# A three-group sigmoid recurrence with ten warm-up steps instead of twelve, the first of them without a product

## The chip, the cores and the metric

The kernel runs on one core of one Trainium2 chip. The metric is the device time of one execution, in microseconds; the median of three runs of the kernel before is 1776.05 (1774.83 to 1778.08).

## The reference, cut to what matters

`x` is 8 images of 128 channels and 48 x 48 = 2304 tokens, all fp32. Layer 0 is group norm, a causal attention over the tokens and a residual; layer 1 normalises the tokens, runs a full attention and adds it. Both attentions are left as they are by the change. What follows them is the feed-forward part, a recurrence over the tokens:

```python
def _L1_ffn_ref(x, W, V, gamma, beta):
    B, T, H = (x.shape[0], x.shape[1], W.shape[0])        # 8, 2304, 128
    Wx = jnp.einsum('bti,hi->bth', x, W)
    flat = Wx.reshape(B * T, H)
    mean = jnp.mean(flat, axis=0); var = jnp.var(flat, axis=0)
    Wx = ((flat - mean) * jax.lax.rsqrt(var + BN_EPS) * gamma + beta).reshape(B, T, H)
    Vt = V.T
    def step(yt, wx_t):
        yt = jax.nn.sigmoid(wx_t + yt @ Vt)
        return (yt, yt)
    y0 = jnp.zeros((B, H), dtype=Wx.dtype)
    _, ys = jax.lax.scan(step, y0, jnp.swapaxes(Wx, 0, 1))
    return jnp.swapaxes(ys, 0, 1)
...
t = t + _L1_ffn_ref(_ln_t(t), L1_ffn_W, L1_ffn_V, L1_ffn_gamma, L1_ffn_beta)
```

`V` is orthogonal, and a sigmoid's slope is at most a quarter, so the state forgets where it began in a few steps.

## The kernel before, in words

There are two parts, one after the other, in the function `fast_path`.

The first part, nearly all of the time, is the two attentions of eight images. TensorE's work is a list, `stream`, written out by hand: for each item a product of scores (L1013 causal, L1214 full), and three items later the product with the values (L1024, L1228, L1224). Between them a small planner, `Stream`, places chains of short steps (projections, norms, transposes, residuals) by stated costs and due times. The schedule is manual: each engine executes its instructions in the order in which they are recorded. The constants of the recurrence come in early. `ffn_weights` (L743 to L751) is one such step, put in with a due time of 30 us: DVE takes the row means off the weights `w1` (L746 to L748), TensorE transposes it into one PSUM bank `tp_ffn` (L750), and DVE copies it out as `w1T` (L751). `vT_f`, the transposed `V`, is loaded from memory (L740).

The second part is the recurrence (L1443 on). The 2304 tokens of each image are cut into 96 segments of LS = 24 tokens, so that all segments of all images go through the 24 steps at once. The 96 segments form G = 3 groups of 32, and a step of one group is a 128 x 256 tile (8 images x 32 segments). A segment doesn't know the state that the one before it ends with, so each starts WARM = 12 tokens earlier, in the tail of the segment before, from a state of 0.5 (`y0`, L1506 and L1507). The step is: DVE writes the scaled inputs of two steps into a PSUM bank (`inputs`, L1488 to L1502: one instruction for groups 1 and 2, and in the warm-up two for group 0, whose first segment has no segment before it); TensorE adds `V y` into the bank (L1547, an fp32 product, so two matmul records); ACT takes the sigmoid out of PSUM (L1549). The three groups take turns on each engine. Group 0's first segment begins at the first token, so its warm-up is discarded: its state is set to 0 (L1552). At the end `seams` (L1515) compares the state at which each segment ends with the warmed-up state at which the next began; if any differs by over 1e-5, a flag sends the program into `general_path`, which computes everything again.

Around the loop: TensorE clears six banks with products of zeros (L1475) and fills a wait with products that nobody reads (`idle`, L1477 and L1395), and makes a small product for the flag (L1533) ahead of the first step. The queue of SP loads the residuals (L1462 and L1464) and later stores the results (L1530). GpSimd adds the residuals (L1529) from step 1 on, and issues adding stores for group 0 (L1562). The last four steps' residuals are added by DVE.

Of the kernel before, what the change touches and what calls it, by code (L numbers as in the profile page):

```python
# [14 lines left out]
F32 = mybir.dt.float32  # L15
AF = mybir.ActivationFunctionType
ALU = mybir.AluOpType
# [8 lines left out]
SEGS = 96  # L26
# [578 lines left out]
def fast_path(ctx: ExitStack, tc: tile.TileContext, x, pe, w_ffn, out, x_tok, w_qkv, w_pos, v_t, gamma_beta, flag):  # L605
    nc = tc.nc
    B, C, H, W = x.shape
    N = H * W
    P = 128
# [15 lines left out]
    LS = N // SEGS  # L625
# [27 lines left out]
    w1T = cpool.tile([P, P], F32, tag="w1T", name="w1T")  # L653
    vT_f = cpool.tile([P, P], F32, tag="vT_f", name="vT_f")
    gb = cpool.tile([P, 2], F32, tag="gb", name="gb")

    def rsqrt(pool, out_ap, var_ap, eps, tag):

# [5 lines left out]
    with ExitStack() as actx:  # L664
# [78 lines left out]
        def ffn_weights():  # L743

            s = small.tile([P, 1], F32, tag="gn_d", name="w_sum")
            nc.vector.tensor_reduce(s, w1, AX.X, ALU.add)  # L746
            nc.vector.tensor_scalar_mul(s, s, 1.0 / P)
            nc.vector.tensor_scalar(w1, w1, s, None, ALU.subtract)  # L748
            tp = psum_t("tp_ffn")
            nc.tensor.transpose(tp[:, 0:P], w1, ident)  # L750
            nc.vector.tensor_copy(w1T, tp[:, 0:P])  # L751


        same = apool.tile([P, R, SQ], F32, tag="same", name="same")
# [685 lines left out]
        order.close()  # L1440


    WARM = 12  # L1443
    G = SEG_GROUPS
    TZ = 2
    TO = [4] + [2] * (G - 1)
    assert LS * SEGS == N and WARM % TZ == 0 and LS % TO[0] == 0 and SG * B * TZ == CH
    with ExitStack() as rctx:
        rc = rctx.enter_context(tc.tile_pool(name="rconst", bufs=1))
        rst = [rctx.enter_context(tc.tile_pool(name=f"rst{g}", bufs=4 if g == 0 else 6)) for g in range(G)]  # L1450
        rres = rctx.enter_context(tc.tile_pool(name="rres", bufs=6))
        rlast = rctx.enter_context(tc.tile_pool(name="rlast", bufs=4))
        ps_z = [rctx.enter_context(tc.tile_pool(name=f"ps_z{g}", bufs=2, space=PSUM)) for g in range(G)]
        ps_w = rctx.enter_context(tc.tile_pool(name="ps_w", bufs=1, space=PSUM))

        rctx.enter_context(tc.manual_schedule())


        t2s = [None] + [rc.tile([P, B, LS, SG], F32, tag=f"t2s_{g}", name=f"t2s_{g}") for g in range(1, G)]
        for g in range(1, G):  # L1460
            for b in range(0, B, 4):
                nc.sync.dma_start(t2s[g][:, b : b + 4], t2s_d[:, g - 1, b : b + 4])  # L1462
        t2l = rc.tile([P, LS - LM, B, SG], F32, tag="t2l", name="t2l")
        nc.sync.dma_start(t2l, t2l_d)  # L1464

        zero = rc.tile([P, CH], mybir.dt.bfloat16, tag="zero", name="zero")
        nc.gpsimd.memset(zero, 0.0)
        pw = ps_w.tile([P, CH], F32, tag="w", name="pw")

        zs = [deque() for _ in range(G)]  # L1470
        banks = [deque() for _ in range(G)]
        for t in range(-WARM, -WARM + 2 * TZ, TZ):
            for g in range(G):
                z = ps_z[g].tile([P, TZ, B, SG], F32, tag="z", name=f"z_{g}_{t}")
                nc.tensor.matmul(z.rearrange("p t b s -> p (t b s)"), zero[:, :P], zero, start=True, stop=True)  # L1475
                banks[g].append(z)
        idle(pw[:, 2 * P :], 8)  # L1477

        mv = rc.tile([P, 2], F32, tag="bn_mv", name="bn_mv")
        nc.vector.bn_aggr(mv, stats)  # L1480
        a = rc.tile([P, 1], F32, tag="bn_a", name="bn_a")
        rsqrt(rc, a, mv[:, 1:2], 1e-5, "bn")
        nc.vector.tensor_mul(a, a, gb[:, 0:1])
        c = rc.tile([P, 1], F32, tag="bn_c", name="bn_c")
        nc.vector.tensor_mul(c, mv[:, 0:1], a)
        nc.vector.tensor_sub(c, gb[:, 1:2], c)

        def inputs(g, t):  # L1488


            z = banks[g].popleft() if banks[g] else ps_z[g].tile([P, TZ, B, SG], F32, tag="z", name=f"z_{g}_{t}")
            s0 = g * SG
            if t >= 0:
                nc.vector.tensor_scalar(z, wx[:, t : t + TZ, :, s0 : s0 + SG], a, c, ALU.mult, ALU.add)
            else:
                before = wx[:, LS + t : LS + t + TZ]
                if g:
                    nc.vector.tensor_scalar(z, before[:, :, :, s0 - 1 : s0 + SG - 1], a, c, ALU.mult, ALU.add)
                else:
                    nc.vector.tensor_scalar(z[:, :, :, 1:], before[:, :, :, : SG - 1], a, c, ALU.mult, ALU.add)  # L1500
                    nc.vector.tensor_scalar(z[:, :, :, 0:1], before[:, :, :, 0:1], a, c, ALU.mult, ALU.add)
            return z  # L1502

        prev, warm, y = [], [], [None] * G
        for g in range(G):
            y0 = rc.tile([P, B, SG], F32, tag=f"y0_{g}", name=f"y0_{g}")  # L1506
            nc.gpsimd.memset(y0, 0.5)  # L1507
            prev.append(y0)
            warm.append(rc.tile([P, B, SG], F32, tag=f"warm_{g}", name=f"warm_{g}"))
            zs[g].append(inputs(g, -WARM))  # L1510

        d = rc.tile([P, G, B, SG], F32, tag="d", name="d")
        dm = rc.tile([P, G], F32, tag="dm", name="dm")

        def seams(g):  # L1515

            n = SG if g < G - 1 else SG - 1
            nc.vector.tensor_sub(d[:, g, :, : SG - 1], prev[g][:, :, : SG - 1], warm[g][:, :, 1:])
            if n == SG:
                nc.vector.tensor_sub(d[:, g, :, SG - 1 :], prev[g][:, :, SG - 1 :], warm[g + 1][:, :, 0:1])  # L1520
            nc.vector.tensor_reduce(dm[:, g : g + 1], d[:, g, :, :n], AX.XY, ALU.max, apply_absolute_value=True)

        ys = {}

        def add_residual(g, l0, yt):
            engine, pool = (nc.gpsimd, rres) if l0 < LM - TZ else (nc.vector, rlast)
            r = pool.tile([P, TZ, B, SG], F32, tag="r", name=f"r_{g}_{l0}")
            t2 = t2s[g].rearrange("p b l s -> p l b s")[:, l0 : l0 + TZ] if g else t2l[:, l0 - LM : l0 - LM + TZ]
            engine.tensor_add(r, yt, t2)  # L1529
            nc.sync.dma_start(out[g, :, l0 : l0 + TZ], r)  # L1530


        nc.tensor.matmul(pw[0:1, :B], ones[:, 0:1], bound, start=True, stop=True)  # L1533
        fl = rc.tile([1, 4], F32, tag="fl", name="fl")
        nc.vector.reduce_max(fl[:, 0:1], pw[0:1, :B], AX.X)
        nc.vector.tensor_scalar(fl[:, 1:2], fl[:, 0:1], LOGIT_BOUND / SCALE, None, ALU.is_gt)

        for t in range(-WARM, LS):
            s = t % TZ
            for g in range(G):  # L1540
                if s == 0 and t + TZ < LS:
                    zs[g].append(inputs(g, t + TZ))
                so = t % TO[g]
                if so == 0:
                    y[g] = rst[g].tile([P, TO[g], B, SG], F32, tag="y", name=f"y_{g}_{t}")
                z = zs[g][0]
                nc.tensor.matmul(z[:, s], vT_f, prev[g], start=False, stop=True, skip_group_check=True)  # L1547
                to = warm[g] if t == -1 else y[g][:, so]
                nc.scalar.activation(to, z[:, s], AF.Sigmoid)  # L1549
                prev[g] = to  # L1550
                if t == -1 and g == 0:
                    nc.vector.memset(warm[0][:, :, 0:1], 0.0)  # L1552
                if s == TZ - 1:
                    zs[g].popleft()

                    l0 = t + 1 - TZ
                    ys[g, l0] = y[g][:, so + 1 - TZ : so + 1]
                    if 0 <= l0 and (g or l0 >= LM):
                        if l0 < LM - TZ:
                            add_residual(g, l0, ys[g, l0])  # L1560
                    elif l0 >= 0 and so == TO[0] - 1:
                        nc.gpsimd.dma_start(out[0, :, t + 1 - TO[0] : t + 1], y[0], accum_op=ALU.add)  # L1562
                if t == LS - 1:
                    seams(g)
                elif t == LM + 1 and g:
                    add_residual(g, LM - TZ, ys[g, LM - TZ])

        off = rc.tile([P, 1], F32, tag="off", name="off")
        nc.vector.tensor_reduce(off, dm, AX.X, ALU.max)
        nc.vector.tensor_scalar(off, off, STATE_TOL, None, ALU.is_gt)  # L1570
        for k, (l0, g) in enumerate((l, g) for l in range(LM, LS, TZ) for g in range(G)):
            add_residual(g, l0, ys[g, l0])
            if k:
                continue
            nc.tensor.matmul(pw[0:1, P : P + 1], off, ones[:, 0:1], start=True, stop=True)
            nc.vector.tensor_scalar(flag, pw[0:1, P : P + 1], fl[:, 1:2], 0.5, ALU.add, ALU.is_gt)
# [56 lines left out]
```

## Time and profile before

| | |
|---|---|
| median of three runs | 1776.05 us (1774.83, 1776.05, 1778.08) |
| profiled execution, first to last instruction | 1772.5 us |
| what lies around it, against that median | 3.58 us |
| TensorE granted clock, mean | 0.993 |
| recurrence, from its first product to the last sigmoid | 1710.25 to 1757.2 us |
| stores and flag after that, to the end | 15.3 us |
| TensorE products L1547 in the warm-up | 12 steps x 3 groups |

Times inside the profile are from the span's start. Each row of the timeline is the start, how long it took, the engine, the line, the operation, the tile written and the tiles read, the number of instructions merged, and in brackets how long the engine had been idle and what released it. PE stands for TensorE, PEld for its weight loads, DVE for VectorE, ACT for ScalarE, POOL for GpSimd, SP for SyncE. The runs' times are of other executions than the profiled one; no time of its own is recorded for that beside its span.

### The profile page before, as it was taken

Reading aid. Unit: us, or ns where it says so; the run is one execution under the profiler, and the core shown is the slowest. Engines: PE = TensorE matmul, PEld = TensorE weight load, DVE = VectorE, ACT = ScalarE, POOL = GpSimd, SP = SyncE. Lnnn points to the kernel's source line nnn. Section 1 sums busy time; section 2 is a strip of 40 time slices with the busy share of each in tenths; the row PEclk is TensorE's granted clock in tenths of the full one; section 3 lists DMA queues with packets and bytes.
Section 4 is the critical chain, followed back from the end, with each engine's and each line's share of the span. In section 5 each row is a group of like instructions: output and inputs, shape, how many; then the busy total and the mean of one; then the engine's idle time right before and its main releaser. Section 6 shows DMA issues by size and latency. Waiting matters only on the chain.

```text
span 1772.5 us, 22223 instructions
## 1 busy us (share of the span) xinstructions
PE 1742.7 (98%) x6231; PEld 1093.2 (62%) x6231; DVE 1302.8 (74%) x3363; ACT 764.8 (43%) x1842; POOL 195.2 (11%) x303
## 2 busy tenths in 40 slices
PE   8999999999999999999999999999999999999996
PEld 5666566665666566665666656665666656665565
DVE  4868668876887668786687767876687866877467
ACT  2344434443345434444344433454344543444455
POOL 1110011100110001100111001100011001110006
PEclk8999999999999999999999999999999999999998
DMA  4405672257533584156732575335941468116768
GB/s 140 138 23 187 182 204 94 87 184 188 145 103 128 159 226 141 34 176 182 200 99 80 188 192 152 106 111 161 237 129 50 160 183 214 45 65 198 194 211 216
DMA packets 206056, 262.00 MB, mean 148 GB/s; under 512 B 90113, under 2 KB 175010, under 8 KB 205412
## 3 DMA queue, kind: packets, MB, share of 16 engines
q1 hardware_dynamic: 204972, 257.47, 49.4%
q0 software_dynamic: 720, 2.62, 1.0%
q8 instruction: 52, 0.85, 0.2%
q14 instruction: 80, 0.66, 0.1%
q10 hardware_dynamic: 232, 0.40, 0.1%
HBM read 150.24 MB, written 110.17 MB: 147 GB/s over the span
## 4 chain that ended last, share of the span: by engine, by line
PE 96%; DMA 1%; DVE 1%; ACT 0%; issue 0%; SPq 0%; POOL 0%; ACTq 0%; POOLq 0%; DVEq 0%
PE o L1228 18%; PE s L1214 18%; PE s L1013 17%; PE o L1024 17%; PE o L1224 13%; PE pj L874 4%; PE pj L877 2%; PE z L1547 2%; PE wx L1320 2%; PE of_t L934 1%; PE tb L934 1%; PE pb L832 0%; DMA x<-in_x_dram 0%; PE dn L1072 0%; PE ts L1259 0%
## 5 line engine op out<-in xcount | busy, mean ns | idle before, releaser
L1216 ACT ACTIVATE p<-s,shift 128x384 f32<-128x384 f32 x504 | 292.4, 580 | 479.7 <-PE s L1214 464.2
L1015 ACT ACTIVATE p<-s 128x384 f32<-128x384 f32 (+2 forms) x504 | 231.8, 460 | 424.8 <-PE s L1013 377.5
L1214 PE MATMUL s<-xh 128*128 128x384 f32 x1008 | 410.4, 489 | 0.0
L1228 PE MATMUL o<-p,xhT 128*128 128x384 f32 x1008 | 404.1, 488 | 5.9 <-ACT p L1216 5.9
L1013 PE MATMUL s<-q,k 128*128 128x384 f32 (+2 forms) x1008 | 381.5, 460 | 0.2 <-DVE k L884 0.2
L1024 PE MATMUL o<-p,vT 128*128 128x384 f32 (+2 forms) x1008 | 377.4, 456 | 0.0
L1224 PE MATMUL o<-g,xhT 128*128 128x384 f32 x720 | 281.3, 488 | 1.1 <-DMA g<-e 1.1
L1228 PEld LDWEIGHTS o<-p,xhT 128*128 128x128 f32 x1008 | 188.9, 190 | 133.8 <-ACT p L1216 10.5
L1024 PEld LDWEIGHTS o<-p,vT 128*128 128x128 f32 x1008 | 188.8, 190 | 114.7 <-issue 0.6
L1214 PEld LDWEIGHTS s<-xh 128*128 128x128 f32 x1008 | 186.2, 190 | 115.3
L1013 PEld LDWEIGHTS s<-q,k 128*128 128x128 f32 x1008 | 182.6, 191 | 97.3 <-issue 1.0
L1039 DVE TENSOR_TENSOR acc<-acc,p 128x384 f32<-128x384 f32 (+2 forms) x408 | 208.8, 512 | 33.4 <-POOL p L1018 8.7
L1177 DVE STREAM_TRANSPOSE t<-p 128x384 f32<-128x384 f32 x360 | 187.3, 550 | 37.6 <-ACT p L1216 32.8
L1224 PEld LDWEIGHTS o<-g,xhT 128*128 128x128 f32 x720 | 133.2, 190 | 83.7 <-DMA g<-e 1.3
L1185 DVE TENSOR_REDUCE tsum<-t 128x12 f32<-128x1152 f32 x120 | 162.3, 1353 | 4.2
L879 DVE TENSOR_TENSOR z<-pj,pb 128x384 f32<-128x384 f32 x144 | 78.8, 547 | 108.8 <-PE pj L874 92.4
L1018 POOL TENSOR_TENSOR p<-p,triu 128x128 f32<-128x128 f32 x144 | 72.5, 505 | 606.2 <-ACT p L1015 475.2
L1294 POOL TENSOR_TENSOR roots<-ve_f,mhalf 128x3 f32<-128x3 f32 x48 | 40.7, 849 | 521.8 <-DVE ve_f L918 521.8
L1216 ACT ACTIVATION_READ_ACCUMULATOR p<-s,shift 128x1 f32 x504 | 97.2, 193 | 0.0
L874 PE MATMUL pj<-xn,wT 128*128 128x384 f32 x192 | 79.7, 500 | 1.4 <-DVE xn L867 1.4
L924 POOL TENSOR_TENSOR rs_c<-ve_c,mhalf 128x3 f32<-128x3 f32 x48 | 45.1, 939 | 216.2 <-DVE ve_c L918 213.6
L1321 DVE TENSOR_TENSOR scale<-wx,scale 128x384 f32<-128x384 f32 x46 | 25.4, 551 | 56.1 <-PE wx L1320 50.3
(264 smaller groups left out, 1485.6 us busy)
## 6 DMA issues: line engine op xcount, KB each, us to landing
e<-t SPq DMA_DIRECT2D x120, 576.0 KB
g<-e SPq DMA_DIRECT2D x480, 144.0 KB
pb<-posb_d SPq DMA_DIRECT2D x46, 576.0 KB
t1t<-in_x_tok_dram SPq DMA_DIRECT2D x48, 192.0 KB
t_d<-tt SPq DMA_DIRECT2D x184, 48.0 KB
t2x<-t_d SPq DMA_DIRECT2D x46, 192.0 KB
scale<-rs SPq DMA_DIRECT2D x46, 192.0 KB
x<-in_x_dram SPq DMA_DIRECT2D x14, 576.0 KB
```

What stands on the lines that cost most here:

```text
L874: nc.tensor.matmul(ps[:, :QC], wT[:, j, :], xn, start=True, stop=True)
L879: nc.vector.tensor_add(z, ps[:, :QC], c["pb"][:, j, :])
L1013: nc.tensor.matmul(s[:, off:QC], keys[b][:, ts(m, P)], queries[b, j][:, off:], start=True, stop=True)
L1015: nc.scalar.activation(p[:, off:], s[:, off:QC], AF.Exp, scale=SCALE)
L1024: nc.tensor.matmul(o[:, off:QC], vals[b][:, ts(m, P)], p[:, off:], start=first, stop=last)
L1039: nc.vector.tensor_add(a[:, off:], a[:, off:], p[:, off:])
L1177: nc.vector.transpose(t[:, :, :, g, :].rearrange("p b j r -> p j b r"), p.rearrange("p (j b r) -> p j b r", j=QB, b=R))
L1185: nc.vector.tensor_reduce(self.tsum[j][:, n - j - 1, :], t.rearrange("p b j m r -> p (b j) (m r)"), AX.X, ALU.add)
L1214: nc.tensor.matmul(s[:, :QC], xh[:, ts(m, P)], xh[:, ts(j, QC)], start=True, stop=True)
L1216: nc.scalar.activation(p, s[:, :QC], AF.Exp, bias=shift, accum_out=self.rows[:, m, j : j + 1])
L1224: nc.tensor.matmul(out_ap, xhT[:, QB * i + g, :], p, start=first, stop=last)
L1228: nc.tensor.matmul(o[:, :QC], xhT[:, what[1], :], p, start=first, stop=last)
```

## The change

The warm-up is ten steps. In its first step, the state before it is a constant, 0.5 in every element, so `V y` is the same column for every token: half the row sums of `V`. That column, `v_half`, is computed once (a product of `vT_f` with a column of 0.5, in the bank `tp_ffn` that the transposed weights also use), copied to SBUF, and given to the first sigmoid as its bias. So the first step has no product, and the three tiles `y0` with their fills are gone. Group 0's warm-up inputs become one instruction: the tile is read one element earlier, so the first segment of each image reads some other element, and what comes of it is discarded as before.

```diff
+    half = cpool.tile([P, 1], F32, tag="half", name="half")
+    nc.gpsimd.memset(half, 0.5)
+    v_half = cpool.tile([P, 1], F32, tag="v_half", name="v_half")
...
             nc.tensor.transpose(tp[:, 0:P], w1, ident)
             nc.vector.tensor_copy(w1T, tp[:, 0:P])
+            nc.tensor.matmul(tp[:, P : P + 1], vT_f, half, start=True, stop=True)
+            nc.vector.tensor_copy(v_half, tp[:, P : P + 1])
...
-    WARM = 12
+    WARM = 10
...
-                before = wx[:, LS + t : LS + t + TZ]
-                if g:
-                    nc.vector.tensor_scalar(z, before[:, :, :, s0 - 1 : s0 + SG - 1], a, c, ALU.mult, ALU.add)
-                else:
-                    nc.vector.tensor_scalar(z[:, :, :, 1:], before[:, :, :, : SG - 1], a, c, ALU.mult, ALU.add)
-                    nc.vector.tensor_scalar(z[:, :, :, 0:1], before[:, :, :, 0:1], a, c, ALU.mult, ALU.add)
+                at = (LS + t) * B * SEGS - 1
+                before = wx.rearrange("p l b s -> p (l b s)")[:, at : at + TZ * B * SEGS]
+                before = before.rearrange("p (l b s) -> p l b s", l=TZ, b=B)[:, :, :, s0 : s0 + SG]
+                nc.vector.tensor_scalar(z, before, a, c, ALU.mult, ALU.add)
...
-            y0 = rc.tile([P, B, SG], F32, tag=f"y0_{g}", name=f"y0_{g}")
-            nc.gpsimd.memset(y0, 0.5)
-            prev.append(y0)
+            prev.append(None)
...
-                if so == 0:
+                if so == 0 or t == -WARM:
                     y[g] = rst[g].tile([P, TO[g], B, SG], F32, tag="y", name=f"y_{g}_{t}")
                 z = zs[g][0]
-                nc.tensor.matmul(z[:, s], vT_f, prev[g], start=False, stop=True, skip_group_check=True)
                 to = warm[g] if t == -1 else y[g][:, so]
-                nc.scalar.activation(to, z[:, s], AF.Sigmoid)
+                if t > -WARM:
+                    nc.tensor.matmul(z[:, s], vT_f, prev[g], start=False, stop=True, skip_group_check=True)
+                    nc.scalar.activation(to, z[:, s], AF.Sigmoid)
+                else:
+                    nc.scalar.activation(to, z[:, s], AF.Sigmoid, bias=v_half)
```

## The prediction

> **What bounds the kernel now.** I read four views: the page's part 4 first (what the end depends on), then the chain of waits over the recurrence, the timeline of the two places that the diff touches, and the busy times by stretch.
>
> The chain that ended last lies on TensorE nearly everywhere, so a TensorE microsecond saved or added anywhere should reach the end, unless a wait takes it up:
>
> ```profile
> PE 96%; DMA 1%; DVE 1%; ACT 0%; issue 0%; SPq 0%; POOL 0%; ACTq 0%; POOLq 0%; DVEq 0%
> ```
>
> The chain at the start of the recurrence (start, length, what):
>
> ```profile
> 1710.19 0.12 PE pw L1533 x2
> 1710.32 0.63 PE z_-12_14294 L1547 x2
> 1710.95 0.44 PE z_-12_14296 L1547 x2
> 1711.44 0.67 PE z_-12_14298 L1547 x2
> 1712.11 0.43 PE z_-12_14294 L1547 x2
> ...
> 1718.69 0.43 PE z_-6_14383 L1547 x2
> 1719.13 0.43 PE z_-6_14389 L1547 x2
> ```
>
> From 1712.11 on, a group's step takes 0.43 us of TensorE, a step of three groups 3 x 0.432 = 1.296 us. TensorE is the limit, not the loop through ACT, which would give 0.59 + 0.38 us. Only the first round is slower (1710.32 to 1712.11, 1.79 us): it waits for DVE's first inputs, as the timeline shows.
>
> ```profile
> 1708.72 0.80 DVE L1500 TENSOR_SCALAR z_-12_14294<-wx,bn_a,bn_c 128x496 f32<-128x496 f32 x1
> 1709.55 0.31 DVE L1501 TENSOR_SCALAR z_-12_14294<-wx,bn_a,bn_c 128x16 f32<-128x16 f32 x1
> 1709.77 0.81 DVE L1498 TENSOR_SCALAR z_-12_14296<-wx,bn_a,bn_c 128x512 f32<-128x512 f32 x1
> 1710.48 0.81 DVE L1498 TENSOR_SCALAR z_-12_14298<-wx,bn_a,bn_c 128x512 f32<-128x512 f32 x1
> ```
>
> DVE's instructions of 0.81 us start 0.71 us apart; group 0's two cost 0.83 + 0.22 us.
>
> The other place is at 30 us, where `v_half` is put. TensorE stands still there already, waiting for DVE's weight means, and its clock then falls:
>
> ```profile
> 28.11 0.49 PE L1013 MATMUL s<-q,k 128*128 128x128 f32 x2
> ...
> 30.09 0.43 PE L750 MATMUL tp_ffn<-ident,w 128*128 128x128 f32 x1 [1.50 <-DVE w L748]
> ...
> 30.56 0.29 DVE L751 COPY w1T<-tp_ffn 128x128 f32<-128x128 f32 x1 [0.52 <-PE tp_ffn L750]
> ```
>
> Busy times by stretch (length; PE, PEld, DVE, ACT, POOL; granted clock, DMA share, GB/s):
>
> ```profile
> 29.00:30.00 1.00, 0.00 (x0) 0.00 (x0) 0.93 (x4) 0.00 (x0) 0.65 (x1) 1.00 1.00 410
> 31.00:32.00 1.00, 1.00 (x3) 0.64 (x2) 0.00 (x0) 0.00 (x0) 0.00 (x0) 0.50 0.36 143
> 1725.00:1730.00 5.00, 5.00 (x24) 4.26 (x23) 4.53 (x8) 4.36 (x12) 0.80 (x1) 1.00 0.00 0
> 1735.00:1740.00 5.00, 5.00 (x25) 4.39 (x24) 4.30 (x7) 4.42 (x13) 5.00 (x6) 1.00 1.14 294
> ```
>
> **What the Trainium skill says.** "TensorE: Matmul & The Clock Gate", Part 1: the clock is halved after an idle window of about 3.4 us and restored after a busy one, and the windows run freely, so their place differs between executions. The trace agrees on the length: the clock is 0.50 from 30.3 to 33.7 us. It is stricter on the cause: 1.5 us without a product was enough here. "ScalarE: Activation LUTs", What ACT_TABLE_LOAD costs: a bias given as a 128 x 1 operand adds about 93 ns to an ACTIVATE. The trace agrees: the exponential with a bias takes 580 ns (L1216, 128x384), the one without 490 ns (L1015's 128x384 form).
>
> **The change part by part.**
>
> 1. *Three rounds of products leave TensorE*: 12 rounds become 9, at 1.296 us: -3.89 us if the new start is as good as steady state.
>
> 2. *The new start.* DVE's chain up to 1708.70 is untouched. Group 0's first input is now one instruction, ready at 1709.53; groups 1 and 2 follow at 1710.24 and 1710.95. ACT can take the first sigmoids straight after these (0.04 us to notice, 0.38 + 0.09 us long): 1710.04, 1710.75, 1711.46. TensorE is not free before 1710.32, since the fillers and L1533 stand ahead of the first product in its queue, so the first product of step -9 starts at 1710.32, just where step -12 started before; group 2's ends at about 1712.2. The next inputs follow on DVE after L1535 and L1536 (two times 0.18 us): from 1711.11 on, ready at 1711.92, 1712.63 and 1713.34. TensorE's second round therefore waits for groups 1 and 2 (1712.75 and 1713.46, a product after a wait lasting 0.67 us, as at 1711.44) and ends at 1714.13. Two rounds on, step -6 begins at 1714.13 + 1.296 = 1715.42. Before, it began at 1718.69. Gain: 3.27 us. So 0.62 of the 3.89 us is given back to DVE's start, and the bias's 3 x 0.09 us lies behind DVE's waits.
>
> 3. *One instruction less per pair of steps on DVE* (1.05 to 0.71 us, 0.34): DVE needs 2.14 us per 2.59 us of TensorE instead of 2.48, so nothing comes of it past the start. If the shifted read were slower than the 0.81 us of groups 1 and 2, which it equals in form, there are 0.45 us of room.
>
> 4. *After the warm-up* all work follows the steps. GpSimd's first addition comes at 1729.20, released by a sigmoid, and is idle before; DMA moves nothing from 1725 to 1730 and the residual loads are in by about 1724, before the first addition's new time of 1725.9. The stores, which then fill the DMA engines, start that much earlier: I pass on all 3.27 us. The three fills of `y0` (0.31 us each on GpSimd) and the fill of `half` lie where GpSimd waits: nothing. No DMA is added or moved, and no queue of SP changes its order.
>
> 5. *`v_half` at 30 us.* In the changed program the new product waits for the copy L751, which reads the same bank, and stands ahead of L874 in TensorE's queue; behind it wait all later products. So: L750 ends at 30.52; 0.04 us to DVE, 0.29 us copy, 0.04 us back: 30.89. The product's two passes with a 128 x 128 weight and one column: the nearest row is the group norm's (L799), 0.56 us on the chain at 10.72, also at half clock. L874 begins at 31.44 instead of 30.52: +0.92 us. Does this pass on? The chain runs from here over TensorE to 43.43, over DVE to 48.04 and over TensorE again; DVE's idle time before 43.45 is a wait for that same L874 of TensorE, so I take all of it. Bounds: 0.21 us (the like product L1072 amid full-clock work: 0.12 us, and 0.09 us more for its successor), if the wait were covered; 0.67 us with the clock full; and above, a second window at half clock, which takes half of 3.41 us, 1.71 us, more. The copy to `v_half` (0.15 us, as L801) lies in DVE's wait for `pb` that ends at 35.98: nothing.
>
> Sum: -3.27 + 0.92 = -2.35 us. The profiled execution goes from 1772.5 to 1770.1 us; with 3.58 us around it, which is how the median stands to it, 1776.05 becomes **1773.7 us**, 0.13% less. The measurement can tell about 0.2% (3.6 us) from no change.
>
> **The rivals.**
>
> (a) *More of it arrives.* Slack somewhere after 30 us takes up the new wait, or the start is smoother: 1776.05 - 3.27 = 1772.8, and at most 1776.05 - 3.89 = 1772.2. For: the exact share of TensorE's records that is waiting can't be read. Against: the chain stays on TensorE from there.
>
> (b) *The clock falls for longer; slower than before.* Its place is 30.3 us. Before, 1.5 us without products, in one window, halved the clock for one window. Now there is the same gap, a 0.43 us transpose, a gap of 0.37 us and a product of one column. If the monitor counts that as idle, two windows may be lost, or the window after it does not count as busy: each costs 1.71 us. From 2.35 / 1.71 = 1.4 further windows on, the kernel is slower; with two it takes 1776.05 - 2.35 + 3.41 = 1777.1. For: at 10 to 20 us the clock stayed at 0.50 for three windows although TensorE was 86 to 100% busy. Against: from 31.44 on L874 and L1013 fill the array, and 2.4 us of such work in a window (16.65 to 19.09) did bring the clock back. One further window gives 1775.4.
>
> (c) *The tail does not move.* If loads or stores ended at their own time, only the cost at 30 us would be left: 1776.05 + 0.92 = 1777.0. Against: the empty DMA engines from 1725 to 1730.
>
> (d) *Ten steps are too few and everything is computed again.* Worked out with the reference's inputs in double precision, the largest seam difference is 7e-9 after 12 steps and 1.4e-7 after 10, against a limit of 1e-5. Negligible.
>
> **How the numbers follow.** The sum: 0.52. (a): 0.24. (b): 0.18, a single further window being most of it. (c) and the rest: 0.06. The range is 1771.4 to 1776.9: (a)'s lower end, less 0.8 us for the spread of the runs (3.25 us among three), to just below (b)'s two windows. Faster by over 0.2% means under 1772.5: half of (a) and a part of the sum's case through the runs' spread, 0.25 together. Slower by over 0.2% means above 1779.6, several lost windows or something not seen: 0.04. The remainder, 0.71, is within 0.2%.
>
> **What would show it.** Part 2: step -9's first product about 1.6 us after DVE's first input begins, and step -6's 6.7 us after it instead of 10.0. Part 4: the time from step -6 to the end stays 53.8 us. Part 5: about 0.9 us between L750's end and L874's start, in which DVE copies and a one-column product runs, and the same shift still there at 48 us. Rival (b): the clock at 0.50 beyond 33.7 us. I am wrong if the main part between 50 us and 1705 us changes its length by over 1 us, which nothing in the diff explains.

## The result and the profile after

The changed kernel takes 1770.82 us (median of 8, 1768.86 to 1772.48), the kernel before 1776.17 us on the same chip (median of 8). The ratio is 0.9974 [0.9965, 0.9984]: 4.6 us less, with 2.8 to 6.2 us inside the interval (the two medians themselves lie 5.35 us apart). The forecast was 2.35 us less, 1773.7 us. Applied to the 1776.05 us of the prediction, the ratio gives 1771.4 us, just at the lower end of the range; the median itself lies 0.6 us below it. So the direction was right, and the size was about half of what was measured.

The profiled execution went from 1772.5 to 1768.1 us. Lines of code below `ffn_weights` are three to six numbers higher than before (L750 is now L753, L1547 is L1550, the first sigmoid is L1553).

The chain that ended last is on TensorE as before (part 4 of the page, changed kernel):

```profile
PE 96%; DMA 1%; DVE 1%; ACT 1%; issue 0%; SPq 0%; POOL 0%; ACTq 0%; DVEq 0%; POOLq 0%
```

The chain at the start of the recurrence, changed kernel (start, length, what):

```profile
1709.86 0.48 ACT y_-10_14348 L1553
...
1710.39 0.70 PE z_-10_14303 L1550 x2
1711.09 0.45 PE z_-8_14305 L1550 x2
...
1711.58 0.67 PE z_-8_14307 L1550 x2
...
1712.30 0.67 PE z_-8_14309 L1550 x2
1712.97 0.43 PE z_-8_14305 L1550 x2
...
1714.26 0.43 PE z_-6_14356 L1550 x2
```

The second round of products has the 0.67 us of a product after a wait (1711.58 and 1712.30); from 1712.97 on there is the steady 0.43 us. Step -6 begins at 1714.26. Who sets the start is seen in the timeline of the changed kernel (start, length, engine, line, operation, tile written and tiles read):

```profile
1707.53 0.81 DVE L1504 TENSOR_SCALAR z_-10_14299<-wx,bn_a,bn_c 128x512 f32<-128x512 f32 x1
1708.25 0.80 DVE L1504 TENSOR_SCALAR z_-10_14301<-wx,bn_a,bn_c 128x512 f32<-128x512 f32 x1
1708.38 0.47 ACT L1553 ACTIVATE y_-10_14342<-z_-10_14299,v_half 128x256 f32<-128x256 f32 x1 [2.07 <-DVE z_-10_14299 L1504]
1708.97 0.80 DVE L1504 TENSOR_SCALAR z_-10_14303<-wx,bn_a,bn_c 128x512 f32<-128x512 f32 x1
1709.03 0.70 PE L1550 MATMUL z_-10_14299<-y_-10_14342,vT_f 128*128 128x256 f32 x2
```

One DVE instruction now fills group 0's bank, the sigmoid follows 0.04 us after it, and the first product starts 1.50 us after DVE's first input began. From that input to step -6 there are 1714.26 - 1707.53 = 6.73 us; before it was 1718.69 - 1708.72 = 9.97 us.

The other place, at 30 us, in the timeline of the changed kernel:

```profile
29.13 0.33 PE L753 MATMUL tp_ffn<-ident,w 128*128 128x128 f32 x1 [1.50 <-DVE w L751]
29.49 0.29 DVE L754 COPY w1T<-tp_ffn 128x128 f32<-128x128 f32 x1 [0.42 <-PE tp_ffn L753]
29.84 0.38 PE L755 MATMUL tp_ffn<-half,vT_f 128*128 128x1 f32 x2 [0.38 <-DVE w1T L754]
30.08 1.60 PE L879 MATMUL pj<-xn,wT 128*128 128x384 f32 x2
```

From the transpose to the projection L879 it is 0.95 us here; the chain of waits puts L879 at 30.22, thus 1.09 us, where it was 0.43 us (30.09 to 30.52). The new product waits for the copy L754, as said, but it runs at full clock for the most part. Busy times by stretch, changed kernel (length; PE, PEld, DVE, ACT, POOL; granted clock, DMA share, GB/s):

```profile
30.00:31.00 1.00, 1.00 (x4) 0.70 (x5) 0.16 (x1) 0.00 (x0) 0.00 (x0) 0.56 0.33 134
31.00:32.00 1.00, 1.00 (x3) 0.52 (x2) 0.00 (x0) 0.00 (x0) 0.00 (x0) 0.50 0.00 0
...
1720.00:1725.00 5.00, 5.00 (x25) 4.26 (x24) 4.22 (x7) 4.38 (x12) 0.24 (x1) 1.00 0.29 117
1725.00:1730.00 5.00, 5.00 (x25) 4.42 (x24) 4.30 (x7) 4.42 (x13) 5.00 (x5) 1.00 0.59 128
```

The clock falls at 30 us to a half as before, for one window (30.12 to 33.54). And between 1725 and 1730 us the DMA engines now move data and GpSimd adds, which they did not before: the tail has moved forward with the steps.

I laid the two traces against each other by the starts of ACT's instructions, which are the same but for the warm-up. Where the 4.4 us of the profiled execution went:

| stretch | change |
|---|---|
| start to the transpose at 30 us (the load of `x` took 6.21 instead of 7.45 us) | -0.96 us |
| `v_half` | +0.85 us |
| 33 to 1679 us | within 0.1 us |
| 1679 us to the recurrence's first DVE input | -1.07 us |
| that input to step -6 | -3.25 us |
| step -6 to the end | +0.04 us |

The first row is scatter: two traces of the kernel before have 7.45 and 6.08 us for the same load. The fourth row is in no part of the prediction. In it the chain holds the load of `t2x` from memory; in the first trace of the kernel before:

```profile
1684.14 4.84 DMA t2x<-t_d
```

and in the changed kernel:

```profile
1683.66 4.26 DMA t2x<-t_d
```

### The profile page after: what moved, and what is told of

Read it like the earlier page. It is cut to its first block, busy times and chain, and to the rows that moved or that the text cites. A ratio compares the mean times of both kernels' runs of the same rounds, so it can differ in the third digit from the quotient of the medians.

```text
span 1768.1 us, 22177 instructions
## 1 busy us (share of the span) xinstructions
PE 1739.9 (98%) x6215; PEld 1092.2 (62%) x6215; DVE 1299.7 (74%) x3355; ACT 762.5 (43%) x1836; POOL 194.9 (11%) x301
## 4 chain that ended last, share of the span: by engine, by line
PE 96%; DMA 1%; DVE 1%; ACT 1%; issue 0%; SPq 0%; POOL 0%; ACTq 0%; DVEq 0%; POOLq 0%
PE o L1233 19%; PE s L1219 19%; PE s L1018 17%; PE o L1029 17%; PE o L1229 13%; PE pj L879 4%; PE pj L882 2%; PE z L1550 2%; PE wx L1325 2%; PE of_t L939 1%; PE tb L939 1%; PE pb L837 0%; DMA x<-in_x_dram 0%; PE dn L1077 0%; PE ts L1264 0%
## 5 line engine op out<-in xcount | busy, mean ns | idle before, releaser
L879 PE MATMUL pj<-xn,wT 128*128 128x384 f32 x192 | 79.9, 501 | 1.4 <-DVE xn L872 1.4
```

The costliest lines, as they stand in the source:

```text
L879: nc.tensor.matmul(ps[:, :QC], wT[:, j, :], xn, start=True, stop=True)
```

## The experiments

The theory was the prediction's: 3.3 us from the recurrence, 0.9 us given back at 30 us. It leaves about 2 us of the result open. The rivals: the new tiles `half` and `v_half` shift the addresses of the tiles after them (by 64 bytes, as I count it; no trace shows an address), and a transfer gains by that; or the cost at 30 us does not arrive at the end; or the recurrence gains more than its trace shows. Each ratio is to the kernel before on the same chip. Diffs are against the kernel before or the changed one, as said.

**Both kernels again.** These two, without an edit, show what repeats.

> The changed kernel once more, beside the three below on one chip, since medians of one kernel differed by 2 us between chips. Theory A (3.2 us gained in the recurrence, 0.8 us lost at 30 us, the rest scatter of the start): 2.4 us less than before, ratio 0.9986. The first measurement's 0.9974 taken at its word: 4.6 us less.

> The kernel before, unchanged, against itself: how far the comparison itself can be off, and a second trace of the stretch from 1679 us to the recurrence, where five of six kernels with moved addresses took 0.7 to 1.5 us less than before. Theory A (scatter): ratio 1.000 +- 0.0005, and that stretch may take 1 us less here too. Theory B (the 64 bytes): ratio 1.000, and that stretch as long as in the first trace of before, within 0.5 us.

The changed kernel: 1770.45 us against 1774.69, 0.9976 [0.9967, 0.9984]. The kernel before against itself: 1.0002 [0.9994, 1.001], 1775.33 against 1775.08. (One of the 33 executions behind that 1775.08 took 5353.63 us. It is not in the ratio, and no trace of it tells why.) In the trace of the first the recurrence takes the same as in the profile after (first input to the first weight load of step -6, which lies 0.37 us ahead of its first product in the chain: 6.36 and 6.35 us; before 9.60 in both traces). The new trace of the kernel before shows something that its first one did not have. Busy times by stretch:

```profile
46.00:48.00 2.00, 1.08 (x2) 0.78 (x3) 1.33 (x4) 0.00 (x0) 0.00 (x0) 0.71 0.00 0
48.00:50.00 2.00, 2.00 (x5) 0.82 (x4) 1.36 (x3) 0.28 (x1) 0.61 (x1) 0.50 0.00 0
```

TensorE waits for DVE up to 46.92 us, about as long as in the first trace. Timeline, the first trace's product and then this one's:

```profile
48.09 0.91 PE L874 MATMUL pj<-xn,wT 128*128 128x384 f32 x2 [1.44 <-DVE xn L867]
...
46.92 1.65 PE L874 MATMUL pj<-xn,wT 128*128 128x384 f32 x2 [1.45 <-DVE xn L867]
```

In this execution, and not in the first, the clock (third from the right, ahead of the DMA share and GB/s) is halved from 46.83 to 50.25 us; it costs this trace 1.6 us against the first (its lead of 1.17 us is a lag of 0.41 us from there on). In traces of other kernels below it was two windows, 3.3 us. "TensorE: Matmul & The Clock Gate", Part 1, of the Trainium skill says that the windows run freely. That would let the same gap count in one execution and not in another; the two traces fit it and differ here by 1.6 us.

**Only the ten steps** (against the kernel before; two steps less, everything else old, with products in the first step):

```diff
-    WARM = 12
+    WARM = 10
...
-                if so == 0:
+                if so == 0 or t == -WARM:
```

> The kernel before with ten warm-up steps and nothing else changed: the product in the first step and the fills of y0 stay, and no address moves ahead of the recurrence. Theory A: two rounds of products less, 2 x 1.296 = 2.6 us less, 1773.6. Theory B gives the same 2.6 us here, but then the changed kernel's further gain must be the addresses. A rival, that the end is set by stores that do not move: no change.

0.9985 [0.9979, 0.9992], 2.7 us less. The recurrence's start took 7.01 us instead of 9.60, 2.59 us less, two rounds of 1.296. The chain of this kernel:

```profile
1712.63 0.63 PE z_-10_14294 L1547 x2
...
1717.13 0.43 PE z_-8_14300 L1547 x2
```

The comparison's 1.4 to 3.7 us hold the trace's 2.59, so what the recurrence saves does arrive at the end (the two medians, 1772.44 and 1774.24, lie 1.8 us apart).

**Two instructions for group 0 again** (against the changed kernel):

```diff
-                nc.vector.tensor_scalar(z, before, a, c, ALU.mult, ALU.add)
+                if g:
+                    nc.vector.tensor_scalar(z, before[:, :, :, s0 - 1 : s0 + SG - 1], a, c, ALU.mult, ALU.add)
+                else:
+                    nc.vector.tensor_scalar(z[:, :, :, 1:], before[:, :, :, : SG - 1], a, c, ALU.mult, ALU.add)
+                    nc.vector.tensor_scalar(z[:, :, :, 0:1], before[:, :, :, 0:1], a, c, ALU.mult, ALU.add)
```

> The changed kernel with group 0's warm-up inputs again in two instructions. By the working of DVE's start: the second round's last input comes 0.67 us later, so step -6 begins 0.67 us later after DVE's first input (7.0 instead of 6.35 us, from the first weight load of that step). Rival (TensorE is the limit from the first product on): no difference, 6.35 us.

One execution, 1769.5 us, which says nothing at this size. The trace does: the start takes 7.01 us instead of 6.35, 0.66 us more. DVE's timeline of this kernel:

```profile
1706.61 0.80 DVE L1505 TENSOR_SCALAR z_-10_14299<-wx,bn_a,bn_c 128x496 f32<-128x496 f32 x1
1707.44 0.31 DVE L1506 TENSOR_SCALAR z_-10_14299<-wx,bn_a,bn_c 128x16 f32<-128x16 f32 x1
...
1711.08 0.81 DVE L1503 TENSOR_SCALAR z_-8_14309<-wx,bn_a,bn_c 128x512 f32<-128x512 f32 x1
```

The last input of the second round starts 1711.08 - 1706.61 = 4.47 us after the first; in the changed kernel it is 3.83 us (1711.36 - 1707.53). As long as TensorE waits for DVE, each instruction counts.

**`v_half` alone** (added to the kernel before; nothing uses it):

```diff
+    half = cpool.tile([P, 1], F32, tag="half", name="half")
+    nc.gpsimd.memset(half, 0.5)
+    v_half = cpool.tile([P, 1], F32, tag="v_half", name="v_half")
...
+            nc.tensor.matmul(tp[:, P : P + 1], vT_f, half, start=True, stop=True)
+            nc.vector.tensor_copy(v_half, tp[:, P : P + 1])
```

> The kernel before with the column v_half computed at 30 us as in the changed kernel, and nobody reading it. Theory A: 0.9 us more than before (1777.1), seen as 0.9 us between the transpose of the weights and the projection behind it, and the same shift at 48 us. Theory B: 1 to 2 us less, since the addresses move. Rival on the clock: half clock for one further window, 2.6 us more, 1778.8.

0.9999 [0.9991, 1.0008], 0.2 us less, from 1.6 less to 1.4 more. The chain of this kernel at 30 us:

```profile
29.34 0.34 PE tp_ffn L753
...
29.71 0.30 DVE w1T L754
...
30.06 0.38 PE tp_ffn L755 x2
30.44 1.38 PE pj L879 x2
```

30.44 - 29.34 = 1.10 us, as in the changed kernel. Against the first trace of the kernel before, ACT's next exponential goes from 0.75 us early to 0.01 us late: 0.76 us, and that stays up to 1679 us. In the single trace the stall passes on whole. Against the kernel before the median does not show it. But this edit adds the two tiles as well, so it moves the addresses too, and its like without the product is `pad` (further on), which ran beside it. There `vhalf_only` has 1774.32 against 1772.98 us, 13 executions each: 1.3 us more by the medians, 0.9 us by the means (0.1 to 1.7 at 95%). So the stall may well be in the median, and a gain by the moved addresses may hide it.

**`v_half` elsewhere.** Twice the product was moved to the start of the recurrence. First into the bank `pw`, ahead of the fillers, with the copy on ACT (against the changed kernel, from which the two lines in `ffn_weights` are taken out):

```diff
+        nc.tensor.matmul(pw[:, P : P + 1], vT_f, half, start=True, stop=True)
+        nc.scalar.copy(v_half, pw[:, P : P + 1])
```

> The changed kernel with v_half computed at the start of the recurrence instead of at 30 us, in the spare bank pw, ahead of the filler products, and copied by ACT, which is idle there. Theory A: the 0.9 us at 30 us goes, and the product's 0.2 to 0.3 us ahead of the fillers is covered by the first sigmoids: 0.8 us less than the changed kernel, 1770.0, 3.2 to 5.5 us less than before depending on the scatter. Rival (the 0.9 us at 30 us is taken up by slack later): same time as the changed kernel, 1770.8.

0.9978 [0.9969, 0.9988]. It made a new wait. The timeline of this kernel:

```profile
1706.07 0.16 ACT L1481 COPY v_half<-pw 128x1 f32<-128x1 f32 x1 [2.33 <-PE pw L1480]
1707.15 1.28 ACT L1553 ACT_TABLE_LOAD   x1 [0.92 <-DVE z_-10_14297 L1504]
...
1708.44 0.47 ACT L1553 ACTIVATE y_-10_14342<-z_-10_14297,v_half 128x256 f32<-128x256 f32 x1
```

The load of the sigmoid's table had lain at 1705.03 us in the changed kernel, with no wait ahead of it. Now it comes after a wait for DVE's first input, and holds the first sigmoid for 1.28 us ("ScalarE: Activation LUTs", What ACT_TABLE_LOAD costs, states 1283 ns, and the trace agrees). Yet step -6 begins only 0.17 us later (6.52 us), since by then all inputs lie ready and the second round waits no more. So this run did not tell of the place at 30 us alone. The second time the product has a bank of its own, and DVE copies it:

```diff
+        ps_v = rctx.enter_context(tc.tile_pool(name="ps_v", bufs=1, space=PSUM))
...
+        pv = ps_v.tile([P, 1], F32, tag="v", name="pv")
+        nc.tensor.matmul(pv, vT_f, half, start=True, stop=True)
...
+        nc.vector.tensor_copy(v_half, pv)
```

> v_half as in the run late, at the start of the recurrence, but in a PSUM bank of its own and copied by DVE while that waits for GpSimd's root, so that ACT's table load stays early. Theory A: the 0.8 us at 30 us is gone and the first sigmoids start as early after DVE's inputs as in the changed kernel: 0.8 us less than the changed kernel in the comparison, 3.2 us less than before; in the trace, step -6 begins 6.7 us after DVE's first input. Rival (the wait at 30 us was hidden): no difference from the changed kernel.

0.9976 [0.9969, 0.9983], the same as the changed kernel run beside it (1770.34 and 1770.45 us). Its recurrence starts in 6.36 us, so nothing new was added there, and the 0.8 us at 30 us that are gone do not show: the changed kernel is 0.1 us quicker by the means, from 1.1 quicker to 0.9 slower. Its trace lost a window at 46.7 to 50.12 us, 1.6 us, which the changed kernel's traces did not.

**A bank of its own at 30 us** (against the changed kernel): the product need not wait for the copy.

```diff
-            nc.tensor.matmul(tp[:, P : P + 1], vT_f, half, start=True, stop=True)
-            nc.vector.tensor_copy(v_half, tp[:, P : P + 1])
+            tv = psum_t("tp_vh")
+            nc.tensor.matmul(tv[:, 0:1], vT_f, half, start=True, stop=True)
+            nc.vector.tensor_copy(v_half, tv[:, 0:1])
```

> The changed kernel with the product for v_half in a PSUM bank of its own, so that it needn't wait for the copy of the weights. By the parts of the forecast's 0.92 us: the wait of 0.37 us goes and the product stays, so the projection behind it begins 0.35 us earlier after the transpose's start than the changed kernel's 1.09 us: 0.7 us. Rival (TensorE would stand still for another reason): 1.1 us.

One execution, 1772.51 us. The chain of this kernel:

```profile
28.34 0.47 PE tp_ffn L753
28.81 0.22 PE tp_vh L756 x2
29.03 1.49 PE pj L880 x2
30.52 1.28 PE s L1019 x2
...
33.08 1.58 PE pb L838 x2
34.66 1.58 PE pj L880 x2
```

From the transpose to the projection it is 0.69 us: the wait is gone and the product costs 0.22 us. But the clock stayed at a half for three windows, 27.86 to 38.1 us. The products at 33.08 and 34.66 take 1.58 us where the kernel with `v_half` alone has 0.84 (34.18 and 35.02); between 33 and 45 us this execution lost 2.8 us against the first trace of the kernel before. Further windows lost at 30 us are what rival (b) feared, here in another kernel and in one trace. That the one-column product is the cause is not shown: the clock fell at 27.86 us, before that product began.

**The gap filled** (`late2`, and products that nobody reads, ahead of the transpose):

```diff
+            idle(tp[:, 2 * P :], 6)
```

> As late2, and six filler products (1.5 us) in front of the transpose of the weights at 28.6 us, where TensorE waits 1.5 us for DVE. If that gap is what halves the clock for the window from 30.3 us on, the window stays at full clock and 1.0 to 1.7 us are gained over late2, less in the mean where the gap straddled two windows anyway. If the clock falls for another reason (the work before it uses 33 rows), no gain and the clock at 0.50 stays.

0.9969 [0.9957, 0.9981], 1769.38 us, 1 us below `late2` beside it, within both intervals. Busy times by stretch of this kernel:

```profile
28.00:30.00 2.00, 1.84 (x8) 1.12 (x7) 0.40 (x2) 0.17 (x1) 0.00 (x0) 1.00 0.73 300
30.00:32.00 2.00, 2.00 (x7) 0.83 (x6) 0.00 (x0) 0.79 (x2) 0.00 (x0) 1.00 0.33 48
```

The clock stays at 1.00 there, so the filled gap and the full clock go together, as the theory says. It is not proof that the gap alone halved it. In two kernels without fillers the clock stayed at 1.00 too: `late`, with a gap of 1.06 us, and `b_warm10`, with the whole gap. Timeline and busy times of `b_warm10`:

```profile
29.32 0.33 PE L750 MATMUL tp_ffn<-ident,w 128*128 128x128 f32 x1 [1.50 <-DVE w L748]
...
30.00:32.00 2.00, 2.00 (x7) 0.87 (x6) 0.00 (x0) 0.49 (x1) 0.00 (x0) 1.00 0.31 122
```

Of the twelve traces without fillers ten have the half clock there, of the two with them (`fill`, `all8`) none.

**Only the addresses** (the kernel before and two tiles of 4 bytes in a row that nobody reads; no product):

```diff
+    half = cpool.tile([P, 1], F32, tag="half", name="half")
+    nc.gpsimd.memset(half, 0.5)
+    v_half = cpool.tile([P, 1], F32, tag="v_half", name="v_half")
+    nc.gpsimd.memset(v_half, 0.5)
```

> The kernel before with two unused 4-byte tiles per partition, filled by GpSimd, which only move all later tiles by 64 bytes as the changed kernel does. Theory A (the gain is 3.2 us in the recurrence less 0.9 us at 30 us, and the 2 to 3 us beyond it are scatter between executions in waits for transfers that the change does not touch): no change, 1776.2 +- 1.3 us, and in its trace the loading of x and the wait for t2x near 1685 us may differ from those before by about 1 us. Theory B (the moved addresses make transfers quicker): 2 to 3 us less, 1773.5, with the wait for t2x near 1685 us shorter by 1 us as in the changed kernel.

0.9992 [0.9984, 1.0]: 1.4 us less, from 0 to 2.8. **And the reverse**, the changed kernel with both columns in bytes behind `gb` that I take to be unused, so that the tiles after them stay where they were:

```diff
-    gb = cpool.tile([P, 2], F32, tag="gb", name="gb")
-    half = cpool.tile([P, 1], F32, tag="half", name="half")
+    gb = cpool.tile([P, 4], F32, tag="gb", name="gb")
+    half, v_half = gb[:, 2:3], gb[:, 3:4]
...
-        nc.sync.dma_start(gb, gamma_beta)
+        nc.sync.dma_start(gb[:, 0:2], gamma_beta)
```

> The changed kernel with the two new columns put into the unused bytes behind gb, so that no address moves. Theory A: as the changed kernel, 4.4 us less than before (0.9976). Theory B (the moved addresses are worth 1.4 us, as the run pad may say): 2.4 to 3 us less (0.9985), the forecast's number, and the stretch from 1679 us on as long as before.

0.9985 [0.9978, 0.9991]: 2.7 us less, where the changed kernel has 4.3 and 4.6. (The quotient of the two medians, 1771.39 and 1775.08, is 0.9979, so the size is uncertain by about a microsecond.) The load of `t2x` in the chain, `pad`:

```profile
1683.61 3.58 DMA t2x<-t_d
```

`noshift`:

```profile
1683.57 4.95 DMA t2x<-t_d
```

and the kernel before, again:

```profile
1684.88 4.92 DMA t2x<-t_d
```

With the tiles where they were, the load takes 4.84 to 5.00 us in all four traces (`b_warm10` is the fourth). With the tiles moved it stands in the chain of nine of ten traces: in seven of them it takes 3.58 to 4.61 us, in the other two, `fill` and `own_bank`, 5.71 and 5.93 us. The chain of `own_bank`:

```profile
1685.59 5.93 DMA t2x<-t_d
```

The whole stretch from 1679 us to DVE's first input changed against the first trace of before by -0.02, +0.39 and +0.45 us in the three other traces that leave the tiles in place, and by -1.46, -1.36, -1.22, -1.07, -0.95, -0.89, -0.75, -0.71, 0.0 and +0.2 us in the ten that move them: a mean of +0.2 (with the first trace's zero) against -0.8 us. It is likely that about 1 us of the result comes from the moved addresses. The same two exceptions and the overlapping intervals keep it from being settled, and why the address would matter was not found.

**A version beyond both** (`fill`, and further): eight warm-up steps, for which I work out a largest seam difference of 3.6e-6 against the limit of 1e-5, and the flag's product and DVE's two instructions taken from the start into a step of the loop.

```diff
-    WARM = 10
+    WARM = 8
...
-        nc.tensor.matmul(pw[0:1, :B], ones[:, 0:1], bound, start=True, stop=True)
-        fl = rc.tile([1, 4], F32, tag="fl", name="fl")
-        nc.vector.reduce_max(fl[:, 0:1], pw[0:1, :B], AX.X)
-        nc.vector.tensor_scalar(fl[:, 1:2], fl[:, 0:1], LOGIT_BOUND / SCALE, None, ALU.is_gt)
...
+                if t == LM + 1 and g == 0:
+                    nc.tensor.matmul(pw[0:1, :B], ones[:, 0:1], bound, start=True, stop=True)
+                    fl = rc.tile([1, 4], F32, tag="fl", name="fl")
+                    nc.vector.reduce_max(fl[:, 0:1], pw[0:1, :B], AX.X)
+                    nc.vector.tensor_scalar(fl[:, 1:2], fl[:, 0:1], LOGIT_BOUND / SCALE, None, ALU.is_gt)
```

> As fill, with eight warm-up steps (the largest seam difference, worked out with the reference's inputs, is then 3.6e-6 against the limit of 1e-5) and the small product and two small DVE instructions for the flag moved from the front of the recurrence into it. Theory A: two rounds less, 2.6 us, and 0.3 us from DVE's inputs of the second round coming earlier: 2.9 us less than fill, 7 to 8 us less than before. A rival, that the stores after the recurrence now bound: under 1 us less than fill.

1768.75 us against 1774.69, 0.9963 [0.9951, 0.9975], 6.6 us less. Its step -6 is already the second round, whose products wait for DVE, so the two kernels are compared at step -4. The first weight loads of that step, `all8` and then `fill`:

```profile
1715.14 0.41 PEld L1548 LDWEIGHTS z_-4_14362<-y_-8_14348,vT_f 128*128 128x128 f32 x2
...
1716.21 0.41 PEld L1553 LDWEIGHTS z_-4_14387<-y_-8_14368,vT_f 128*128 128x128 f32 x2
```

From DVE's first input (1709.02 and 1707.26) that is 6.12 and 8.95 us: 2.83 less, where 2.9 were expected. Two rounds are 2.59 us of it, and the other 0.24 came with DVE's two small instructions, which no longer stand ahead of the second round. The median beside `fill` is only 0.6 us lower, with 6 and 8 executions, so the 2.8 us are the trace's and not shown in the median. The trace itself lost two half-clock windows, from 46.85 to 53.68 us.

## Why the prediction was partly right

1. *Three rounds, and 2. the new start.* Right. Forecast 6.7 us from DVE's first input to step -6, measured 6.73; the gain forecast at 3.27 us is 3.25. The first product came 1.50 us after that input (forecast 1.6), and the second round waited for groups 1 and 2 with the two products of 0.67 us that were named. (The text says "two rounds on" where its sum rightly adds one.) The bias costs ACT 0.09 us per sigmoid, 0.47 against 0.38 us, as the price in the prediction said, and hides behind DVE.

3. *One instruction for group 0.* "Nothing comes of it past the start" holds. But the start is where TensorE waits for DVE, and there it is worth 0.66 us (`a_two`). The forecast has this inside part 2, which counts one instruction for group 0, without giving its worth.

4. *The tail.* Right. From step -6 to the end (from its first weight load, which is why it is more than the forecast's 53.8) it took 54.16 us before and 54.2 after; rival (c) falls. In the other kernels it was 53.8 to 55.1.

5. *`v_half`.* The wait for the copy is there, and in single traces the stall costs about what was forecast. From the transpose to 55 us, the five traces with it (`own_bank` aside) take 0.81 to 0.88 us more than the first trace of the kernel before; the forecast was 0.92. The product took 0.38 instead of 0.55 us in four of them, and 0.59 in `a_two`, where the clock was already halved. Open is "so I take all of it", the step from one execution to the median. `vhalf_only` against `pad` says 0.9 us [0.1, 1.7], the changed kernel against `late2` says -0.1 us [-1.1, 0.9]. The first agrees with the plain cost, the second just leaves room for it.

A possible reason for the second lies in the clock. Of the eight traces without the stall, four lost one or two windows at 47 us; of the five with it none did. Such a split comes by chance once in ten times. Four of these eight also kept the full clock at 30 us, which gives some 0.7 us back. For the six of them without fillers, the stretch from the transpose to 55 us changed against the first trace of the kernel before by -0.7 to +2.6 us, 0.8 on the average, about the size of the stall. This is a suggestion and not shown.

*The sum.* What is missing in it is a term that it put at nothing, about -1 us between 1679 us and the first DVE input. The prediction said: "I am wrong if the main part between 50 us and 1705 us changes its length by over 1 us, which nothing in the diff explains." It did change, by 1.07 us. Something in the diff may explain it, two tiles of 4 bytes, which the prediction counted as a fill that costs nothing and not as a change of every address behind them. `noshift`, which takes just that away, gives 2.7 us [1.6, 3.9], near the forecast's 2.35. A single trace does not carry this: in the trace of `noshift` the same part became 1.0 us longer with no address moved, so a change of 1 us alone can be scatter. What there is for the addresses is the fourteen traces taken together and the medians of `pad` and `noshift`, and that makes it likely, not shown. With -3.25 for the recurrence, -1.4 for `pad` and +0.8 at 30 us the sum is -3.85 us, inside the measured interval of -6.2 to -2.8; without the 0.8 it is -4.65, the result. Between these two the runs do not decide.

*The time around the span.* The 3.58 us set one execution's span against the median of others. In the changed kernel's profiled execution it is 1769.93 - 1768.1 = 1.83 us with both from one execution, so the profiled execution of before was probably some 1.7 us quicker than the median. It cancels in the difference.

*Rivals.* (a) asked for more to arrive, and its time was nearest, but not by the slack that it named. (b) did not happen in the changed kernel, whose clock is as before (halved from 30.12 to 33.54 us; in the first trace of the kernel before from 30.19 to 33.60). `own_bank` shows that three windows can be lost there, not that the product is the reason. Nor is 1.5 us without a product always enough to halve the clock, as the prediction read from its one trace: in `b_warm10` it was not. (d) did not happen.

## What to carry to other kernels

When an engine waits for another at a start, count every instruction of the other one up to the second round: that working held to 0.03 us. A stall seen in one trace is not yet a cost of the median when a half-clock window of 1.6 us can come or go beside it: test it alone, with enough executions. Adding even a 4-byte tile can move what is allocated after it, so a control with the tile and without its use belongs to any comparison of a few microseconds. `vhalf_only` looks like no cost against the kernel before, and like 0.9 us against `pad`.

## What the runs showed that I had not expected

The half-clock windows come and go between executions of one program, each worth 1.6 us (none at 47 us in the first trace of before, one in the second), after a TensorE gap of 1.45 us in both. A product with one column in two passes takes 0.22 to 0.38 us at 30 us in five traces and 0.59 in `a_two`, where the prediction had 0.55. Waiting for the copy out of the shared bank costs as much again as the product: 0.38 us, read from the gap between L753 and L755. And with the tiles moved the load of `t2x` took 3.6 to 4.6 us in seven traces and 5.7 and 5.9 in two, instead of 4.8 to 5.0 in all four without; the reason stays open.
